# 31 short warming matmuls in place of 15 long ones ahead of a graph-attention kernel

## The chip, the cores and the metric

The kernel runs on one core of a Trainium2 chip. The metric is the device time of one execution in microseconds (us). A TensorE "record" below is one instruction of TensorE as the profile lists it: a weight load (LDWEIGHTS, shown under PEld) or a matmul (MATMUL, shown under PE). A matmul of the program on 32-bit floats comes out as two weight loads and two matmuls, so as four records.

## The reference

The input `x` is 128 graphs of 128 nodes with 768 features, `adj` a 128x128 weighted adjacency per graph. Everything is float32.

```python
h = jnp.maximum(_layernorm(x, axis=-1), 0.0)
x = x + _L0_gnn_ref(h, adj, L0_gnn_Wq, L0_gnn_bq, L0_gnn_Wk, L0_gnn_bk, L0_gnn_Wv, L0_gnn_bv, L0_gnn_beta)
...
q = _split_heads(input_graph @ Wq + bq)
k = _split_heads(input_graph @ Wk + bk)
v = _split_heads(input_graph @ Wv + bv)
scores = jnp.einsum('bhqd,bhkd->bhqk', q, k) / jnp.sqrt(jnp.asarray(HD, input_graph.dtype))
adj_e = adj[:, None, :, :]
scores = scores + beta * adj_e
scores = jnp.where(adj_e > 0, scores, jnp.asarray(-9000000000000000.0, scores.dtype))
probs = jax.nn.softmax(scores, axis=-1)
out = jnp.einsum('bhqk,bhkd->bhqd', probs, v)
```

There are 12 heads of 64 features (`HD`), and `_split_heads` gives each head its own axis.

## The kernel before, in words

The 128 graphs are worked in 32 groups of four (`G` = 0 to 31). For each group there are three "slices" of projections: `qk0` (queries and keys of heads 0 to 5), `v`, and `qk1` (the other queries and keys). In group 0 the projections are plain matrix products (`plain_slice`, line 1048, its first row `first_row`, line 1265). From group 1 on a slice is made of 15 block products (`PRODUCTS`) and each of these of seven inner products (`product`, line 681), every one issued as two matmuls that write the upper and the lower 64 partitions. The right-hand sides of these products were added up once at the start (`prepare`), are kept in DRAM, and are streamed back in a ring of six buffers (`load_T`, the tiles `T_qk` and `T_v`); ten of them stay resident. VectorE, ScalarE and GpSimd add the products up (line 704 and following), decode them, and do masks, exponentials and divisions. The scores (line 776) and the weighting of the values (line 855) of one group are woven between the products of the next.

The order of the work is written out: a table of due times (`TABLE`, with `FIRST`, `SECOND`, `LAST` for the ends) is counted in products, 45 to a group, and every group from the second on issues the same list of instructions on each engine. So TensorE's program is one long list without loops, in which the same stretch comes again once per group.

The change lies at the very start. `direct` first issues the loads of the first two graphs and the weights, and GpSimd writes a 128x128 identity into `ident`. Then `fill(WARM)` puts matmuls of the identity with itself into one PSUM bank, whose result nobody reads: they keep TensorE busy until the first normalised row is there. `rows_1` takes the statistics of a graph on VectorE (line 1089 and following) and `rows_2` scales its row (line 1107), transposes it on TensorE (line 1112), puts one or two more matmuls of `fill` behind each transpose (`FILL`), and takes the result away on ScalarE (line 1118). After that come the products of the first row (line 1265).

Of the kernel before, what the change touches and what calls it, by code (L numbers as in the profile page):

```python
# [18 lines left out]
P = 128  # L19
# [12 lines left out]
@with_exitstack  # L32
def kernel(
    ctx: ExitStack,
    tc: tile.TileContext,
    x: bass.AP,
    adj: bass.AP,
    wq: bass.AP,
    bq: bass.AP,
    wk: bass.AP,  # L40
    bk: bass.AP,
    wv: bass.AP,
    bv: bass.AP,
    beta: bass.AP,
    out: bass.AP,
):

    nc = tc.nc
    keep = ctx.enter_context(tc.tile_pool(name="keep", bufs=1))
    bad = keep.tile([1, 1], I32, name="bad")
    args = (x, adj, wq, bq, wk, bk, wv, bv, beta, out)
    direct(tc, *args, bad)
    again = nc.values_load(bad[0:1, 0:1])
    with tc.If(again > 0):
        general(tc, *args)  # L60
# [43 lines left out]


SC_AT = 1
WARM = 15
FILL = (1, 1, 2)


# [116 lines left out]
def direct(ctx, tc, x, adj, wq, bq, wk, bk, wv, bv, beta, out, bad):  # L227
# [10 lines left out]
    nc = tc.nc  # L238
    B, N, D = x.shape
    HD = D // HEADS  # L240
# [30 lines left out]
    def flat(lo, hi):  # L271
        return sbig[:, lo:hi]
# [32 lines left out]
    ident = flat(spot, spot + P)  # L305
# [772 lines left out]
    def rows_1(g, h):  # L1078

        t = xg[0, g].rearrange("p b f -> p (b f)")
        if not h:
            first["st", g] = stat.tile([P, 2, nc.vector.BN_STATS_DIM], F32, tag="strow_0", name=f"strow0_{g}", bufs=2)
        s = first["st", g]
        with ExitStack() as behind:
            if g:
                behind.enter_context(tc.issue_after(first[("ve", "dve")[h]].ins))
            nc.vector.bn_stats(s[:, h, :], t[:, h * VH:(h + 1) * VH])
        if not h:  # L1090
            return None
        mv = stat.tile([P, nc.vector.BN_AGGR_DIM], F32, tag="mvrow_0", name=f"mvrow0_{g}", bufs=2)
        nc.vector.bn_aggr(mv, s)
        ve = stat.tile([P, 1], F32, tag="verow_0", name=f"verow0_{g}", bufs=2)
        first["ve"] = nc.vector.tensor_scalar(ve, mv[:, 1:2], EPS, None, op0=ALU.add)
        r = stat.tile([P, 1], F32, tag="rsrow", name=f"rsrow_{g}", bufs=2)
        nc.gpsimd.tensor_tensor(r, ve, nhalf, ALU.pow)
        return mv, r

    def rows_2(g, mv, r, ks=range(3)):  # L1100

        v = xg[0, g].rearrange("p b (c j) -> p c b j", c=NC)
        for k in ks:
            if not k:
                first["rows", g] = work.tile([P, 3, 2, P], F32, tag="e", name=f"rows_{g}", bufs=EB)
            n = first["rows", g][:, k]
            first["dve"] = nc.vector.tensor_scalar(n.rearrange("p c (b j) -> p c b j", b=NB), v[:, 2 * k:2 * k + 2], mv[:, 0:1], r, op0=ALU.subtract,
                                                   op1=ALU.mult)
            bank = take()
            p = bank[:, 0, 0:H2].rearrange("p (c i) -> p c i", c=2)  # L1110
            for c in range(2):
                nc.tensor.transpose(p[:, c, :], n[:, c, :], ident)
            if not g:
                fill(FILL[k])
            if not g:
                home_A(0, f"A0{k}")
            t = A[0, f"A0{k}"][:, :, g * N:(g + 1) * N]
            first["relu"] = nc.scalar.activation(t, p, AF.Relu)
            give(bank)


    warm = take()

    def fill(count):
        for _ in range(count):
            nc.tensor.matmul(warm[:, 0, 0:P], ident, ident, start=True, stop=True)

    fill(WARM)
    got = [rows_1(0, h) for h in range(2)]
    rows_1(1, 0)  # L1130
    rows_2(0, *got[1])
# [369 lines left out]
```

## Time and profile before

| What | Value |
|---|---|
| time, median of 3 runs | 2667.34 us (2666.55 to 2667.99) |
| span of the profiled execution, first to last instruction | 2664.1 us |
| what the median has beyond that span | 3.2 us |
| TensorE busy | 2644.1 us, 99% of the span, 52041 matmuls and as many weight loads |
| VectorE, ScalarE, GpSimd busy | 81%, 66%, 79% |
| mean rate of the DMA engines | 277 GB/s |
| mean granted TensorE clock | 0.998 |

The profile gives one execution; it has no time of its own beside the span, so the 3.2 us are what lies before the first and after the last instruction, as far as that execution and the median are alike. Matmuls are pipelined, and the end of one is modelled: a matmul that is listed with 273 ns is followed by the next one long before. The step from start to start is what counts. "Idle before" is the time in which the engine had nothing in hand, with what ended it; "issue" stands where no semaphore explains it.

### The profile page before, as it was taken

What the parts mean: (1) busy time and instruction counts of PE and PEld (TensorE: products, weight loads), DVE (VectorE), ACT (ScalarE), POOL (GpSimd) and SP (SyncE); (2) the same over time, 40 slices, a digit from 0 to 9 for tenths busy, and PEclk for the clock granted to TensorE, in tenths of its full rate; (3) what the DMA queues carried; (4) which work ended last, traced back from release to release, by engine and by line L of the source; (5) the groups of instructions that cost most, each with busy time, mean ns of one, the idle gap of its engine ahead of it and who ended that gap; (6) DMA issues with size and microseconds to landing.
All of it is one profiled execution on the core that took longest, in us unless ns stands there. A gap on an engine that the chain in (4) does not pass through costs nothing.

```text
span 2664.1 us, 121442 instructions
## 1 busy us (share of the span) xinstructions
PE 2644.1 (99%) x52041; PEld 2564.2 (96%) x52041; DVE 2165.8 (81%) x2702; ACT 1755.1 (66%) x4608; POOL 2097.8 (79%) x3043
## 2 busy tenths in 40 slices
PE   9999999999999999999999999999999999999998
PEld 8799999999999999999999999999999999999997
DVE  7878887878888788887788887888877888778876
ACT  2567766677666677666777666776667776667654
POOL 5877778877779777788777797777887777887774
PEclk9999999999999999999999999999999999999999
DMA  8899999998989999999999899999899898999885
GB/s 254 276 281 279 282 284 278 283 292 267 293 281 279 287 277 284 281 281 280 289 269 288 281 281 282 288 275 285 279 278 292 268 291 279 276 286 282 256 253 165
DMA packets 531572, 736.65 MB, mean 277 GB/s; under 512 B 106444, under 2 KB 371160, under 8 KB 531032
## 3 DMA queue, kind: packets, MB, share of 16 engines
q1 hardware_dynamic: 530384, 728.06, 88.5%
q8 instruction: 411, 6.73, 1.0%
q14 instruction: 129, 1.06, 0.1%
q10 hardware_dynamic: 648, 0.79, 0.1%
HBM read 662.22 MB, written 66.51 MB: 274 GB/s over the span
## 4 chain that ended last, share of the span: by engine, by line
PE 94%; DVE 1%; DMA 0%; issue 0%; ACT 0%; SPq 0%; DVEq 0%; ACTq 0%
PE pair L681 80%; PE pair L776 7%; PE pair L855 6%; PE pair L1048 1%; DVE home L704 0%; DMA x<-in_x_dram 0%; DMA T_qk<-kept_qk 0%; PE pair L926 0%; DVE e L789 0%; DVE prep_qk L403 0%; ACT e L836 0%; DVE res_qk L403 0%; PE pair L947 0%; DVE e L931 0%; ACT e L933 0%
## 5 line engine op out<-in xcount | busy, mean ns | idle before, releaser
L704 DVE TENSOR_TENSOR home<-home,pair 128x896 f32<-128x896 f32 x836 | 880.0, 1077 | 220.5 <-PE pair L681 179.8
L681 PE MATMUL pair<-sbig,T_qk 128*64 128x128 f32 x13020 | 827.6, 274 | 2.3 <-DVE home L704 1.2
L681 PEld LDWEIGHTS pair<-sbig,T_qk 128*64 128x64 f32 x13020 | 702.5, 137 | 19.9 <-issue 12.1
L739 POOL TENSOR_TENSOR home<-home 128x256 f32<-128x256 f32 x308 | 266.1, 864 | 320.0 <-DVE home L704 319.7
L681 PE MATMUL pair<-T_v,sbig 128*64 128x128 f32 x7812 | 457.8, 273 | 1.6 <-ACT home L716 0.6
L681 PE MATMUL pair<-A,T_qk 128*64 128x128 f32 x6944 | 445.6, 273 | 0.9 <-issue 0.9
L681 PEld LDWEIGHTS pair<-T_v,sbig 128*64 128x64 f32 x7812 | 430.7, 137 | 8.4 <-ACT e L836 4.8
L855 PE MATMUL pair<-v,e 128*64 128x65 f32 x6048 | 403.5, 221 | 0.0
L836 ACT ACTIVATE e<-e,sm 128x64 f32<-128x64 f32 x1512 | 381.7, 341 | 7.4 <-DVE sm L824 6.1
L681 PEld LDWEIGHTS pair<-A,T_qk 128*64 128x64 f32 x6944 | 384.6, 137 | 1.5 <-issue 1.5
L855 PEld LDWEIGHTS pair<-v,e 128*64 128x64 f32 x6048 | 362.2, 137 | 3.2
L724 ACT ACTIVATE home<-pair 128x640 f32<-128x640 f32 x340 | 240.6, 708 | 188.5 <-PE pair L681 187.2
L681 PE MATMUL pair<-sbig,res_qk 128*64 128x128 f32 x4340 | 312.3, 273 | 0.4
L742 POOL TENSOR_TENSOR home<-home 128x256 f32<-128x256 f32 x308 | 269.7, 876 | 24.1
L885 ACT ACTIVATE sm<-pair,tiny 128x8 f32<-128x8 f32 x189 | 50.8, 269 | 329.5 <-PE pair L855 329.5
L789 DVE SCALAR_TENSOR_TENSOR e<-pair,biasT 128x1024 f32<-128x1024 f32 x189 | 229.4, 1214 | 34.1 <-PE pair L776 33.0
L740 POOL TENSOR_TENSOR home<-home 128x256 f32<-128x256 f32 x308 | 228.2, 741 | 24.1
L681 PEld LDWEIGHTS pair<-sbig,res_qk 128*64 128x64 f32 x4340 | 238.0, 137 | 1.4 <-DVE home L704 1.3
L560 ACT ACTIVATE x<-x,block 128x192 f32<-128x192 f32 x480 | 222.6, 540 | 0.0
L726 ACT ACTIVATE home<-pair,bqk 128x128 f32<-128x128 f32 x680 | 214.3, 377 | 0.0
L798 ACT ACTIVATE e<-e 128x1024 f32<-128x1024 f32 x189 | 196.1, 1055 | 21.8 <-DVE e L789 14.0
L741 POOL TENSOR_TENSOR home<-home 128x128 f32<-128x128 f32 x308 | 175.6, 570 | 24.2
(208 smaller groups left out, 4401.6 us busy)
## 6 DMA issues: line engine op xcount, KB each, us to landing
T_qk<-kept_qk SPq DMA_DIRECT2D x713, 448.0 KB
T_v<-kept_v SPq DMA_DIRECT2D x372, 448.0 KB
xo<-in_x_dram SPq DMA_DIRECT2D x190, 256.0 KB
out_dram<-xo SPq DMA_DIRECT2D x189, 256.0 KB
x<-in_x_dram SPq DMA_DIRECT2D x248, 192.0 KB
sbig<-in_x_dram SPq DMA_DIRECT2D x116, 384.0 KB
kept_qk<-prep_qk SPq DMA_DIRECT2D x23, 448.0 KB
adj<-in_adj_dram SPq DMA_DIRECT2D x128, 64.0 KB
```

Source lines behind the costliest of these rows:

```text
L560: nc.scalar.activation(t, t, AF.Relu, bias=shift[G, n], scale=rstd[G, n])
L681: nc.tensor.matmul(p[q:q + HD, at, :], lhs[:, q:q + HD], rhs, start=(first and at % 4 == 0), stop=True, skip_group_check=True)
L704: nc.vector.tensor_tensor(t, t, p[:, 0:7], op)
L724: nc.scalar.activation(t[:, 0:5], p[:, 0:5], AF.Copy, scale=float(sign))
L726: nc.scalar.activation(t[:, at], p[:, at], AF.Identity, bias=bqk[:, of, oc:oc + 1], scale=float(sign))
L739: e.tensor_tensor(t[:, 1:4:2], t[:, 1:4:2], twice(5), ALU.add)
L740: e.tensor_tensor(t[:, 2:5:2], t[:, 2:5:2], twice(1), ALU.add)
L742: e.tensor_tensor(t[:, 0:7:6], t[:, 0:7:6], twice(2), ALU.add)
L789: nc.vector.scalar_tensor_tensor(e[:, :, at], ps[:, :, at], SCORE_CAP * ISCALE, bias[:, :, at], op0=ALU.min, op1=ALU.add)
L798: nc.scalar.activation(e, e, AF.Exp, scale=1.0 / ISCALE)
L836: nc.scalar.activation(o[:, r, b, 0:HD], pa[:, r, b, 0:HD], AF.Copy, scale=t[:, 1, r, b:b + 1])
L855: nc.tensor.matmul(pa[q:q + HD, 2 * g + i, :], k[:, q:q + HD], vt[G, "v", r, h // 4][:, 4 * g + h % 4, :], start=True, stop=True, skip_gro ...
```

## The change

`WARM` goes from 15 to 31, `fill` gets a width, and the first call uses 64 columns (`HD`) where it had 128 (`P`). The weights of each of these matmuls are still the whole 128x128 identity. The calls `fill(FILL[k])` in `rows_2` keep 128 columns. In records: 31 times 4 are 124, in place of 60, so that everything that TensorE runs later stands 64 records further along in its program.

```diff
-WARM = 15
+WARM = 31
 FILL = (1, 1, 2)
...
-    def fill(count):
+    def fill(count, width=P):
         for _ in range(count):
-            nc.tensor.matmul(warm[:, 0, 0:P], ident, ident, start=True, stop=True)
-
-    fill(WARM)
+            nc.tensor.matmul(warm[:, 0, 0:width], ident, ident[:, 0:width], start=True, stop=True)
+
+    fill(WARM, HD)
     got = [rows_1(0, h) for h in range(2)]
```

## The prediction, as it was put on record

> **What bounds the kernel now.** I read the page first: the engine table, the clock row, the DMA queues, and the chain that ended last.
>
> ```profile
> span 2664.1 us, 121442 instructions
> PE 2644.1 (99%) x52041; PEld 2564.2 (96%) x52041; DVE 2165.8 (81%) x2702; ACT 1755.1 (66%) x4608; POOL 2097.8 (79%) x3043
> ...
> PEclk9999999999999999999999999999999999999999
> ...
> q8 instruction: 411, 6.73, 1.0%
> ...
> PE 94%; DVE 1%; DMA 0%; issue 0%; ACT 0%; SPq 0%; DVEq 0%; ACTq 0%
> ```
>
> TensorE (PE) sets the time: 99% busy, 94% of the chain, at full clock. So the change can act in two ways only: through when TensorE gets through its first microseconds, and through anything that hangs on where an instruction stands in TensorE's list. The row of q8 speaks for the second. This queue moved 411 packets of 6.73 MB / 411 = 16.4 KB, of kind "instruction", and TensorE ran 104082 matmuls and weight loads: 253 for each packet, 256 once its semaphore instructions are counted. I take q8 for TensorE's own program, fetched in blocks of 256 records.
>
> Then the long view of the chain, in order of time. The same stretch of 284 matmuls opens every group; six of these rows:
>
> ```profile
> 171.94 15.65 PE pair L681 x284
> ...
> 1063.68 15.65 PE pair L681 x284
> 1145.49 15.65 PE pair L681 x284
> ...
> 1552.26 15.65 PE pair L681 x284
> ...
> 2120.69 15.65 PE pair L681 x284
> ...
> 2527.99 15.65 PE pair L681 x284
> ```
>
> The first eleven groups take (1063.68 - 171.94) / 11 = 81.07 us each, the last eighteen (2527.99 - 1063.68) / 18 = 81.35 us, though every group issues the same list. The later ones lose 0.28 x 18 = 5.1 us. The timeline of weight loads shows where most of it goes: breaks put down to "issue", with no semaphore behind them. Breaks of 0.17 us that come back in every group are left aside; of the others none lies before 1134 us in a full group.
>
> ```profile
> 1134.82 0.13 PEld L776 LDWEIGHTS pair<-home 64*64 64x64 f32 x1 [0.49 <-issue]
> ...
> 1199.04 0.63 PEld L681 LDWEIGHTS pair<-A,T_qk 128*64 128x64 f32 x12 [0.54 <-issue]
> ...
> 1298.21 0.79 PEld L681 LDWEIGHTS pair<-T_v,sbig 128*64 128x64 f32 x14 [0.25 <-issue]
> ...
> 1443.49 0.79 PEld L681 LDWEIGHTS pair<-A,T_qk 128*64 128x64 f32 x14 [0.48 <-issue]
> ...
> 1606.36 0.74 PEld L681 LDWEIGHTS pair<-A,T_qk 128*64 128x64 f32 x13 [0.43 <-issue]
> ...
> 1949.48 0.52 PEld L681 LDWEIGHTS pair<-T_v,sbig 128*64 128x64 f32 x9 [0.28 <-issue]
> ...
> 2193.71 0.41 PEld L681 LDWEIGHTS pair<-T_v,sbig 128*64 128x64 f32 x7 [0.49 <-issue]
> ...
> 2356.34 0.35 PEld L681 LDWEIGHTS pair<-T_v,sbig 128*64 128x64 f32 x6 [0.18 <-issue]
> ...
> 2438.52 0.42 PEld L681 LDWEIGHTS pair<-T_v,sbig 128*64 128x64 f32 x8 [0.39 <-issue]
> ```
>
> They sum to 3.53 us. What lies between two of them, counted by stretches (start and end, sum, then busy time and count of PE and PEld, VectorE, ScalarE, GpSimd, clock, DMA share, GB/s), and the semaphore instructions on TensorE's main line:
>
> ```profile
> 1134.84:1199.02 64.18, 63.80 (x1265) 62.30 (x1265) 52.69 (x61) 42.92 (x107) 52.94 (x77) 1.00 0.91 278
> 1199.06:1298.20 99.14, 99.14 (x2027) 96.96 (x2028) 80.18 (x99) 68.38 (x187) 78.21 (x113) 1.00 0.92 282
> 1443.52:1606.34 162.82, 162.54 (x3293) 159.21 (x3293) 133.22 (x159) 111.48 (x294) 131.28 (x189) 1.00 0.92 281
> ...
> L681 PEldq EVENT_SEMAPHORE  x990: 51/51/1724, 120.0 to 2645.6; - x198
> ```
>
> There are 990 semaphore instructions in 2526 us, so about 0.4 per us. That makes 2530 + 25, 4055 + 39 and 6586 + 64 records: 2555, 4094 and 6650, against 10, 16 and 26 times 256 (2560, 4096, 6656). The breaks stand at one place modulo 256: they are boundaries of blocks, at which the next block was not yet there. One packet of q8 lies in the 1.2 us from 1132.3 us, just ahead of the break at 1134.82:
>
> ```profile
> q8 instruction: 1, 0.02, 5.0%
> ```
>
> **The change part by part.** First the 32 more matmul records and 32 more weight loads of the fill. The rows, from the timeline of the first 21 us, the source view of the fill, and the chain:
>
> ```profile
> 1.49 5.80 PE L1126 MATMUL pair<-sbig 128*128 128x128 f32 x30 [1.49 <-POOL sbig masks.py:199]
> 7.62 0.20 PEld L1112 LDWEIGHTS pair<-sbig,rows 128*128 128x128 f32 x2 [0.52 <-DVE rows L1107]
> 7.62 0.44 PE L1112 MATMUL pair<-sbig,rows 128*128 128x128 f32 x2 [0.33 <-DVE rows L1107]
> 9.22 1.06 PE L1265 MATMUL pair<-A,sbig 128*128 128x128 f32 x8
> 20.45 0.29 PE L475 MATMUL pair<-st,sbig 128*64 128x16 f32 x4 [1.04 <-DVE st L464]
> ...
> L1126 PE MATMUL pair<-sbig x38: 274/421/582, 1.5 to 9.1; 128*128 128x128 f32 x38
> ...
> 107.81 0.23 PE pair L855 x8
> ```
>
> Once warm, eight matmuls of 128 columns start within 1.06 - 0.275 us, 0.112 us apart (0.275 being the shortest of one, 274 ns). The fill's 30 take 5.80 us, 0.19 us each, since most run at half speed (median 421 ns against 274). Half the columns should take half the step, if the weight load (128 columns as before) fits into it. By itself such a load takes about 0.06 us: the two of line 1112 span 0.20 us, of which the second is some 0.14. That is just the warm half step of 0.056 us, and the rows of 65 columns run at 0.23 / 8 = 0.029 us each, two at a time, 0.058 us a step. So 62 half steps are 31 of the old steps: one more than 30, by 0.11 us if warm. The fill would end near 7.4 in place of 7.29 us. TensorE then stands idle until 7.62 us, when VectorE's scaled row comes (0.33 us), and this covers it: cost 0. If the cover were gone, the first transpose would be late, and behind it lines 1118 and 1265. Upper end: weight load and matmul one after the other, as long as a whole old step. Then 62 steps take 2 x 5.80 us or rather less, as the clock opens after the same 4.5 us: 21 slow ones in 4.4 us, 41 at 0.112 us in 4.6 us, an end at 10.5 us, 2.9 us late. The wait at 20.45 us for line 464, which goes by VectorE and a load, takes 1.04 of that, the one of 0.33 us is already in it: at most +1.9 us. A gain here is excluded: nothing waits for the end of the fill but a row that comes later.
>
> Second, the 64 records. They move every block boundary 64 records up the schedule. A group is 81.05 us or about 13 blocks, so a record is 81.05 / 13 / 256 = 0.0244 us on average, and the boundary comes 1.56 us earlier in the work. Where do the breaks stand within a group? 1199.04 - 1145.49 = 53.55 us in one, 1606.36 - 1552.26 = 54.10 us five groups later: 0.11 us of drift a group. At the other place 1134.82 - 1063.68 = 71.14 and 2193.71 - 2120.69 = 73.02 us, thirteen groups on: 0.14 us a group. At some 0.12 us a group, 1.56 us are 13 groups. So group G will have its boundaries where group G - 13 has them now. The two bad places are entered in the twelfth and thirteenth of the 29 groups; they will be entered 13 groups later. Of the nine breaks, the four up to 1443.49 us (0.49 + 0.54 + 0.25 + 0.48 = 1.76 us) come back, at the end of the run; the five from 1606.36 on (1.77 us) fall off it. Bounds of this term: -1.8 by the rows; if all the 5.1 us are such breaks, half of it, -2.6.
>
> The price is that the first 13 groups put their boundaries where none has been. Each group has 13 of them, so 169 fetches are at unvisited places, against 29 x 13 = 377 that cost 3.53 us: at that mean 1.6 us. To do better than the mean I look at what a bad place is: few microseconds for the 256 records of a block, while the DMA engines are full. Five blocks of a group without breaks, two bad ones first, then the three shortest or fullest of those newly visited:
>
> ```profile
> 300.88:306.28 5.40, 5.40 (x128) 5.22 (x128) 4.91 (x6) 5.08 (x10) 1.70 (x3) 1.00 1.00 341
> 318.15:323.61 5.46, 5.46 (x133) 5.12 (x128) 2.17 (x5) 3.71 (x12) 4.99 (x9) 1.00 0.98 324
> 303.79:309.44 5.65, 5.65 (x134) 5.65 (x132) 5.10 (x8) 5.29 (x15) 3.39 (x4) 1.00 1.01 372
> 322.19:327.85 5.66, 5.66 (x134) 5.49 (x128) 3.69 (x5) 5.48 (x15) 5.19 (x9) 1.00 0.94 300
> 292.28:297.71 5.43, 5.43 (x130) 5.09 (x128) 5.43 (x6) 5.37 (x16) 5.12 (x6) 1.00 0.92 276
> ```
>
> Bad are 5.40 and 5.46 us at a DMA share of 1.00 and 0.98. Only the third is as full (1.01), and it leaves 0.2 us more, which takes away about half of a break of 0.2 to 0.5 us; the fourth and fifth are less full. I take +1.0 us: one place, some 0.15 us in half of 13 groups. Lower end 0; upper end a new place that breaks in all 13 groups by 0.5 us, +6.5.
>
> Sum: 0 - 1.8 + 1.0 = -0.8 us. On the span that is 2663.3; the median lies 3.2 us above the span of the profiled execution, which the change doesn't touch: **2666.5 us**, 0.03% less. What a measurement of this kernel can tell from no change is about 0.2%, 5.3 us.
>
> [...]
>
> **The rivals.** (a) All breaks go and no new ones come: -3.5 by the rows, -5.1 by the groups' lengths, 2662.2 to 2663.8 us. For it: eleven groups run without any. Against: blocks as short as the bad ones lie among the new places. (b) The other side: the block that ends 56 us into a group (303.79 to 309.44) is late in all of the first 13 groups, at 0.3 to 0.5 us: +3.9 to +6.5, less 1.8: 2669.4 to 2672.0, and over 2672.7 only if the block at 322.19 joins it. It decides as soon as the fetch takes 0.2 us longer there than at the bad places. For it: the fullest DMA share of all; against: the longer block. (c) The fill gets longer, because the weight load doesn't fit into the half step, or the clock opens later for short matmuls: up to +1.9 - 0.8: 2668.4 us. Against: the rows with 65 columns. (d) Blocks are always there in time, the breaks hang on something else in the later part of the run, and the shift moves nothing: 2667.3 us. Against: the counts. [...]
>
> **How the numbers follow.** Forecast (net -2.5 to +1.5): 0.68. (a) 0.14, (b) 0.10, (c) 0.04, (d) 0.04. Range: down to 2662.5 for (a), up to 2671.0 for most of (b). Faster by over 0.2% is below 2662.0, just past the far end of (a), with the scatter of the median (0.7 us to either side) some of it: 0.06. Slower is above 2672.7, the part of (b) with both blocks: 0.06. The rest, 0.88, is no change.
>
> **What would show it.** Fill: 62 matmuls at line 1126 that end by 7.6 us, line 1112 still starting at 7.62 with a wait for VectorE. Fetch: breaks by "issue" at the two old places (53.6 and 71.1 us into a group) only from the 25th of the 29 groups on, at most four or five; few or small ones near 56 us in the first 13 groups; all a multiple of 256 records apart. Groups at 81.05 us where there is no break. It is wrong if breaks stay at the same groups as now, if a new place breaks in nearly every group, or if the median leaves the range.

## The result, and the profile after

The changed kernel takes 2673.36 us (median of 13 runs, 2670.75 to 2675.08), the kernel before 2667.74 us beside it (13 runs, 2666.49 to 2669.09): a ratio of 1.0019, 95% interval 1.0011 to 1.0027, so 5.6 us slower. The forecast of 2666.5 us was wrong in its sign, and its range of 2662.5 to 2671.0 us doesn't hold the time. The two profiled executions differ by 2670.6 - 2664.1 = 6.5 us in their spans, and this is what has to be found. It is 0.9 us more than the medians show: in every run with a span on record the time is 1.7 to 1.9 us above it, so the execution of before that was profiled took about 2665.9 us, 1.8 less than the median here, and the changed one, with 2672.43 us, 0.9 less than its own. (Of the 3.2 us that were taken for time outside the span, only some 1.8 are that.)

First the page of the changed kernel: span, engines, the instruction queue and the chain that ended last.

```profile
span 2670.6 us, 121506 instructions
PE 2650.7 (99%) x52073; PEld 2572.3 (96%) x52073; DVE 2164.7 (81%) x2702; ACT 1755.1 (66%) x4608; POOL 2097.8 (79%) x3043
...
q8 instruction: 412, 6.75, 1.0%
...
PE pair L681 80%; PE pair L776 7%; PE pair L855 6%; PE pair L1126 1%; PE pair L1265 0%; POOL prep_qk L386 0%; POOL prep_qk L385 0%; DVE home L704 0%; DMA sbig<-in_L_gnn_Wk_dram 0%; DMA kept_qk<-prep_qk 0%; DVE prep_qk L403 0%; POOL A L590 0%; POOL prep_v L385 0%; POOL prep_v L386 0%; POOL rstd L496 0%
```

TensorE still sets the time, and its busy time has grown by the whole difference, 2650.7 - 2644.1 = 6.6 us, with 32 matmuls more. VectorE, ScalarE and GpSimd work as long as before. The chain of before could be followed back only to 93.8 us, so the first part of this one can't be compared with it. In order of time it begins with line 1126, the fill, which holds 1%. It goes on through the first row on TensorE until 31 us and through the preparation on VectorE and GpSimd (the lines 403, 385 and 386), and is back on TensorE at 134 us; so what is late at the start is handed on through the preparation.

Now the timeline of TensorE's matmuls in the first 29 us. Columns: start, length, engine, line, operation, tile, number of matmuls in a row, and in brackets the idle time ahead of it.

```profile
1.49 13.49 PE L1126 MATMUL pair<-sbig 128*128 128x64 f32 x62 [1.49 <-POOL sbig masks.py:199]
14.77 0.64 PE L1112 MATMUL pair<-sbig,rows 128*128 128x128 f32 x2
...
17.76 1.76 PE L1265 MATMUL pair<-A,sbig 128*128 128x128 f32 x8
19.35 0.38 PE L1112 MATMUL pair<-sbig,rows 128*128 128x128 f32 x2
...
20.68 1.06 PE L1265 MATMUL pair<-A,sbig 128*128 128x128 f32 x8
...
28.38 0.29 PE L475 MATMUL pair<-st,sbig 128*64 128x16 f32 x4
```

The fill takes 13.49 us for 62 matmuls of half the columns, where it took 5.80 us for 30 whole ones. The last one has 0.42 us (421 ns, below), so the step is (13.49 - 0.42) / 61 = 0.214 us; it is 0.213 to 0.214 us from the second step to the last. The first transpose (line 1112) starts at 14.77 us instead of 7.62, 7.15 us late, with no wait ahead of it: the row from VectorE has long been there, and the transpose waits for the fill. The row behind it runs slowly too: line 1265 takes 1.76 us for eight matmuls at 17.76 us and 1.06 us at 20.68 us, as it did at once before. The trace's first record of full speed for TensorE's clock stands at 19.22 us, in place of 6.11 us in the kernel before; the matmuls show the same change of speed between the rows of 17.76 and 19.35 us. (The granted clock of a stretch is listed as 1.00 also ahead of the first record, so here the steps have to be read, not that column.) So the fill is long and it doesn't warm. By line 475 the delay is 28.38 - 20.45 = 7.93 us; it was 21.57 - 12.54 = 9.03 us at the last transpose of the first row, and line 475's wait for VectorE, 1.04 us, has gone into it.

The source view of line 1126, by length of one instruction in ns (shortest, median, longest), first of the kernel before, then of the changed one; and line 1112 before:

```profile
L1126 PEld LDWEIGHTS pair<-sbig x38: 190/333/333, 1.5 to 9.0; 128*128 128x128 f32 x38
...
L1112 PEld LDWEIGHTS pair<-sbig,rows x12: 138/142/143, 7.6 to 12.5; 128*128 128x128 f32 x12
```

```profile
L1126 PEld LDWEIGHTS pair<-sbig x70: 286/333/337, 1.5 to 17.3; 128*128 128x128 f32 x70
L1126 PE MATMUL pair<-sbig x70: 421/421/473, 1.5 to 17.5; 128*128 128x64 f32 x62, 128*128 128x128 f32 x8
```

Matmuls of 64 columns are as long as those of 128, 421 ns in the median, and the weight load is as long as ever, 333 ns at the low speed. At line 1126 it is listed with 190 ns at full speed and 333 ns at the low one, but at line 1112, at full speed, with 138 to 143 ns, the load from which the prediction took its price.

Last, the later part. The stretch of 284 matmuls that opens a group, in the chain in order of time, and the breaks at block boundaries from the timeline of the weight loads:

```profile
179.75 15.65 PE pair L681 x284
...
342.28 15.65 PE pair L681 x284
...
1073.14 15.65 PE pair L681 x284
...
2370.13 15.65 PE pair L681 x284
2453.27 15.65 PE pair L681 x284
2535.06 15.65 PE pair L681 x284
```

```profile
236.14 0.13 PEld L681 LDWEIGHTS pair<-sbig,res_qk 128*64 128x64 f32 x1 [0.30 <-issue]
...
399.21 0.13 PEld L855 LDWEIGHTS pair<-v,e 128*64 128x64 f32 x1 [0.59 <-issue]
...
2425.39 1.17 PEld L681 LDWEIGHTS pair<-A,T_qk 128*64 128x64 f32 x21 [1.71 <-issue]
...
2507.39 1.07 PEld L681 LDWEIGHTS pair<-A,T_qk 128*64 128x64 f32 x20 [0.75 <-issue]
```

The changed kernel is 179.75 - 171.94 = 7.81 us behind at the first of these places, 1073.14 - 1063.68 = 9.46 us at the twelfth and 2535.06 - 2527.99 = 7.07 us at the thirtieth. So the first eleven groups lost 1.65 us, the later eighteen won 2.39 us back, and between the first place and the thirtieth the changed kernel won 0.74 us. New breaks stand 236.14 - 179.75 = 56.4 and 399.21 - 342.28 = 56.9 us into a group, early in the run; the old places, 2425.39 - 2370.13 = 55.3 and 2507.39 - 2453.27 = 54.1 us in, are reached in the 28th and 29th. What the change costs is made in the first 20 us of the run.

That these breaks are late fetches can be read from the packets. The largest ends at 2425.39 us. One packet of q8 lies in the stretch from 2423.0 to 2424.1 us, and none from there to the end of the break:

```profile
q8 instruction: 1, 0.02, 5.2%
```

By the packets' times in the trace it landed at 2423.98 us, 1.41 us before TensorE went on. The four breaks of 0.3 us and more here, and eight of the nine that the prediction lists for the kernel before (all but the one of 0.18 us), end 1.3 to 1.7 us after their block's packet has landed; at the boundaries without a break TensorE enters the block 3.4 to 3.5 us after that in the median.

### The profile page after: what moved, and what is told of

The parts are those of the page before. It is cut to its first block, busy times and chain, and to the rows that moved or that the text cites. A ratio compares the mean times of both kernels' runs of the same rounds, so it can differ in the third digit from the quotient of the medians.

```text
span 2670.6 us, 121506 instructions
## 1 busy us (share of the span) xinstructions
PE 2650.7 (99%) x52073; PEld 2572.3 (96%) x52073; DVE 2164.7 (81%) x2702; ACT 1755.1 (66%) x4608; POOL 2097.8 (79%) x3043
## 3 DMA queue, kind: packets, MB, share of 16 engines
q14 instruction: 129, 1.06, 0.1%
## 4 chain that ended last, share of the span: by engine, by line
PE 95%; POOL 2%; DVE 2%; DMA 1%; issue 1%; ACT 0%; SPq 0%; DVEq 0%; POOLq 0%; ACTq 0%
PE pair L681 80%; PE pair L776 7%; PE pair L855 6%; PE pair L1126 1%; PE pair L1265 0%; POOL prep_qk L386 0%; POOL prep_qk L385 0%; DVE home L704 0%; DMA sbig<-in_L_gnn_Wk_dram 0%; DMA kept_qk<-prep_qk 0%; DVE prep_qk L403 0%; POOL A L590 0%; POOL prep_v L385 0%; POOL prep_v L386 0%; POOL rstd L496 0%
## 5 line engine op out<-in xcount | busy, mean ns | idle before, releaser
L681 PEld LDWEIGHTS pair<-sbig,T_qk 128*64 128x64 f32 x13020 | 703.0, 137 | 19.7 <-issue 12.1
```

The source lines that it names most:

```text
L681: nc.tensor.matmul(p[q:q + HD, at, :], lhs[:, q:q + HD], rhs, start=(first and at % 4 == 0), stop=True, skip_group_check=True)
```

## The experiments

Theory A: the weight load of 128 columns sets the step of a matmul with fewer columns, 0.213 us at the low speed, and an array that streams half of the time doesn't open the clock; the shift of 64 records does next to nothing. Rival B: the start is small, and the shift costs the time. Rival E: load and matmul go in turns, so that the step is their sum. F and G stand for two views of the breaks: F, a place in a group decides whether the fetch of a block is late; G, it is chance.

**The shift alone.** The fill of before; in group 0, in the wait ahead of line 475, 16 matmuls of one column whose result nobody reads, 64 records.

```diff
+        for _ in range(16 if G == 0 else 0):
+            nc.tensor.matmul(bank[0:1, 1, 0:1], ident[:, 0:1], ident[:, 0:1], start=True, stop=True)
```

> The fill is the old one (15 of 128 columns); 16 matmuls of one column with one column of weights, 64 records, stand later, where TensorE waits 1.04 us at line 475 about 20 us into the run. So every block boundary of all full groups lies as in the changed kernel. Theory A (the loss of 5.6 us is made in the fill, the shift alone is worth -0.7 us, the 7.81 to 7.07 us by which the changed kernel is behind at 172 us and at 2528 us): 2667.0 us, within 2666 to 2668; breaks where the changed kernel has them, in the first 9 groups about 56 us into the group and two large ones in the last two. Theory B (the loss is made by the shifted block boundaries): 2673 us.

Measured: 2664.89 us against 2665.98, ratio 0.9998 (0.9988 to 1.0008). The chain of this kernel at the same three places (line 681 stands at 683 here):

```profile
172.20 15.65 PE pair L683 x284
...
1066.13 15.65 PE pair L683 x284
...
2528.06 15.65 PE pair L683 x284
```

The first eleven groups take 893.93 us, 2.2 more than before, the later eighteen 1461.93 us, 2.4 less: the same exchange as in the changed kernel, and nothing is left of it at the end. B falls; what costs is the fill. The expected breaks came at the expected places (56.4 and 56.9 us into two of the first groups, 54.0 and 72.3 us into two late ones), but also 74.8 to 76.1 us into three of the first eleven groups, 0.32 to 0.62 us each, where the changed kernel has none.

**What sets the step.** Three fills of 31 with the same shift of 64 records: 128 columns, 32 columns, and 64 columns with weights of only 64 columns.

```diff
-WARM = 15
+WARM = 31
```

> 31 matmuls of the old 128 columns, 124 records: the same shift as in the changed kernel, a longer fill, but a dense one. Theory A: the clock opens near 6.1 us as before, 21 steps of 0.213 and 41 of 0.112 us end at 10.6 us, first transpose 3.0 us late, 1.1 us given back at 20.45 us: +1.9 us at 172 us, the shift -0.7 us: 2668.9 us, less than the changed kernel although twice the columns are streamed. Theory D (the number of matmuls or records ahead of the row counts, whatever their width): as the changed kernel, 2673 us.

```diff
-    fill(WARM, HD)
+    fill(WARM, 32)
```

> As the changed kernel, but 32 columns in each of the 31 matmuls. Theory A (the load of 128 columns of weights alone sets the step at half clock): step 0.213 us again, the fill ends at 14.7 us as with 64 columns, and the clock opens some 4.5 us after the first dense matmuls, near 19 us: about 2672 us. Theory E (load and matmul take turns: 0.107 us for the load, 0.053 us for 32 columns): step 0.160 us, the fill ends at 11.4 us.

```diff
-            nc.tensor.matmul(warm[:, 0, 0:width], ident, ident[:, 0:width], start=True, stop=True)
+            nc.tensor.matmul(warm[0:width, 0, 0:width], ident[:, 0:width], ident[:, 0:width], start=True, stop=True)
```

> 31 matmuls of 64 columns as in the changed kernel, but each with 64 columns of weights instead of 128. Theory A (the load of 128 columns of weights sets the step of 0.213 us, and a matmul of half that length leaves the array half idle): load and matmul are both halved, the step is 0.107 us and dense, the clock opens near 6 us, the fill ends near 7.3 us: no loss in the first 172 us, the shift -0.7 us: 2667.0 us. Theory E (a weight load and a short matmul take turns, whatever their length): step 0.107 us for the matmul and 0.05 to 0.107 us for the load in turn, 0.16 to 0.21 us, the fill ends at 11 to 14 us and the clock opens late: 2670 to 2673 us.

Measured, as the fill stands in the timeline and in the source view, for 128 columns, for 32, and for the half weights:

```profile
1.49 8.52 PE L1126 MATMUL pair<-sbig 128*128 128x128 f32 x62 [1.49 <-POOL sbig masks.py:199]
9.85 0.38 PE L1112 MATMUL pair<-sbig,rows 128*128 128x128 f32 x2
```

```profile
1.49 13.44 PE L1126 MATMUL pair<-sbig 128*128 128x32 f32 x62 [1.49 <-POOL sbig masks.py:199]
14.74 0.67 PE L1112 MATMUL pair<-sbig,rows 128*128 128x128 f32 x2
```

```profile
1.50 6.34 PE L1126 MATMUL pair<-sbig 128*64 128x64 f32 x62 [1.50 <-POOL sbig masks.py:199]
7.77 0.44 PE L1112 MATMUL pair<-sbig,rows 128*128 128x128 f32 x2
...
L1126 PEld LDWEIGHTS pair<-sbig x70: 138/227/232, 1.5 to 9.2; 128*64 128x64 f32 x62, 128*128 128x128 f32 x8
```

A quarter of the columns takes as long as half of them, 13.44 against 13.49 us, so it is the load alone that sets the step, and E falls: with load and matmul in turns the 32 columns would have been shorter. With whole streams the same 62 loads end after 8.52 us, five us sooner than the "short" ones, because the clock opens (at 4.33 us by its record, sooner than the 6.1 us expected) and the step falls from 0.213 to 0.111 us. With half the weights the step is 0.107 and then 0.058 us, and the fill ends at 7.84 us: only here do half the columns take half the step. The times: 2666.54 us for the whole columns (ratio 1.0001, 0.9991 to 1.001), 2664.22 us for the half weights (0.9994, 0.9984 to 1.0003), 2674.23 us for the 32 columns (one run). So what the change cost is gone once the weights are halved with the columns, and neither the kernel with whole columns nor the one with half weights can be told from the kernel before.

**What opens the clock.** The count of before with 64 columns, and 31 of 96 columns:

```diff
-    fill(WARM)
+    fill(WARM, HD)
```

> 15 matmuls of 64 columns, 60 records as before the change, no shift. Theory A (a matmul of 64 columns behind a whole weight load takes the same 0.213 us as one of 128, and such a fill does not open the clock, which opens some 4.5 us after the first dense matmuls): 30 steps end near 7.9 us, 0.3 us late; the clock stays at half until about 12.4 us; first transposes and products lose about 1.9 us more, the wait at 20.45 us takes 1.1 back: +1.1 us, 2668.8 us. Theory C (only the length of the fill counts, not the clock): +0.3 us that the wait takes back, 2667.7 us. If a step were really half as long, the fill would end at 4.7 us and the clock would be the question alone.

```diff
-    fill(WARM, HD)
+    fill(WARM, 96)
```

> 96 columns in each of the 31 matmuls. Theory A: step 0.213 us at half clock, with the array streaming for 0.160 of it. Theory E: 0.267 us. On the clock: if it opens by how much of the time the array streams, and three quarters are enough, it opens near 6 us and the kernel is where 31 of 128 columns was (fill until 9.7 us, 1.1 us behind at 172 us); if three quarters are not enough, it opens near 19 us as with 64 columns (7.8 us behind).

The timelines, of 15 with 64 columns and of 31 with 96:

```profile
1.49 6.67 PE L1126 MATMUL pair<-sbig 128*128 128x64 f32 x30 [1.49 <-POOL sbig masks.py:199]
7.95 0.63 PE L1112 MATMUL pair<-sbig,rows 128*128 128x128 f32 x2
```

```profile
1.49 9.67 PE L1126 MATMUL pair<-sbig 128*128 128x96 f32 x62 [1.49 <-POOL sbig masks.py:199]
10.99 0.38 PE L1112 MATMUL pair<-sbig,rows 128*128 128x128 f32 x2
```

At the low speed both have the step of 0.213 us, which is also the step of whole columns, so by an estimate from these equal steps the array streams 64 / 128 = 50% and 96 / 128 = 75% of the time. At 75% the clock opens at 6.77 us; at 50% it hasn't opened when the fill ends, the first transposes take 0.63 us as in the changed kernel, and it opens at 11.86 us, 3.9 us after whole streams have begun. In the changed kernel that was 19.22 - 14.77 = 4.45 us. The short fill alone would not show that half streams fail to open the clock, since whole streams took up to 6.2 us to do it (last section); the 13 us of the changed kernel and of the 32 columns do. The two kernels also part the two factors. 15 half streams cost little: 2667.3 us, ratio 1.0005 (0.9995 to 1.0014), 0.75 us behind at the place of 171.9 us. 31 at 75% cost 2.20 us there (2670.24 us, one run). Only many loads, all of them at the low speed, cost 7.8.

Does a half-streamed array also close a clock that is open? And what is the warming worth at all? Two more, each one run:

```diff
     fill(WARM)
+    fill(31, HD)
```

> The 15 matmuls of 128 columns first, as before, and then the 31 of 64 columns. If a half-streamed array only fails to open the clock but doesn't close it, the second part goes at 62 steps of 0.111 us: an end at 7.3 + 6.9 = 14.2 us, the first transpose at 14.3, the row behind it at full speed (line 1265 at 15.9), and the place of 171.9 us at about 177.5 (14.3 - 7.6, less the 1.0 of line 475's wait). If the half-streamed array closes the clock again, steps of 0.213 us come back within the second part, its end is up to 20.5 us, and the place is at 178 to 185. If instead the slow steps of the changed kernel had nothing to do with the clock, the steps are 0.213 us from the first of the second part on: an end at 20.5 us.

```diff
-WARM = 15
+WARM = 0
```

> No warming matmuls at all. By the theory the first row then runs at half speed, as in the changed kernel, but starts at 7.6 us: line 1112 takes 0.6 instead of 0.44 us, line 1265 1.76 instead of 1.06, in all 1.9 us later at 12 us (9.0 - 7.15 of the changed kernel), of which the wait at line 475 gives back about 1.0: the place of 171.9 us at 172.8, and the whole 1 us (plus what the 60 records in the other direction do to the fetch, up to 1 either way) above the kernel before. So the changed kernel, with the place at 179.7, would be 7 us worse than no warming at all. If the late start of the clock did not matter, the place is at 171.9.

The timelines, with both fills (line 1265 stands at 1266) and with none:

```profile
1.49 12.31 PE L1126 MATMUL pair<-sbig 128*128 128x128 f32 x92 [1.49 <-POOL sbig masks.py:199]
...
15.20 1.06 PE L1266 MATMUL pair<-A,sbig 128*128 128x128 f32 x8
```

```profile
7.35 1.12 PE L1112 MATMUL pair<-sbig,rows 128*128 128x128 f32 x4 [5.06 <-DVE rows L1107]
...
9.97 1.56 PE L1265 MATMUL pair<-A,sbig 128*128 128x128 f32 x8
```

Once open, the clock stays open through the half streams: 92 matmuls with 92 loads end sooner than the 62 of the changed kernel (13.80 against 14.98 us), and the row behind them runs at full speed. But for one step of 0.058 us, where the two parts meet, the short ones step 0.110 to 0.113 us there: at full speed, too, a load of 128 columns sets the step. So the changed kernel's steps of 0.213 us are that load with the clock closed. This kernel stands 4.96 us behind at the place of 171.9 us, which was forecast as 5.6; its program is shifted by 124 records against the kernel before, and with that its first eleven groups lose 5.5 us, of which the later eighteen win 3.2 back (see below). It takes 2672.67 us.

Without any fill the place is 0.82 us behind (0.9 was expected), and the kernel takes 2667.9 us in the one run. The warming of before earns at most that 0.8 us; that of the changed kernel loses 7.8 against it.

**What the fetch does, with the boundaries held.** A group has 3323 records, five short of 13 blocks of 256 (the trace of before has 104082 matmuls and loads and 1114 semaphore instructions of TensorE for 411 packets of q8, 256 to a packet); a matmul of one column in each group makes 3327, so that the boundaries stay at nearly one place. Its result is overwritten. The second kernel has 49 matmuls of one column more at 20 us, so that the boundaries are held at a bad place.

```diff
+        if sl == "qk0" and G > 1 and n == order_of(G, sl)[0]:
+            nc.tensor.matmul(p[0:1, 0, 0:1], b[:, 0, 0:1], b[:, 0, 0:1], start=True, stop=True, skip_group_check=True)
```

> The kernel before with one more matmul of one column (4 records, about 0.06 us) at the start of each of the 30 groups from the third on. A group then has 3327 records in place of 3323, against 13 blocks of 256 = 3328, so that the boundaries of the blocks hardly move from group to group and stay where the first groups have them, which ran without breaks. Theory F (the breaks are late blocks of TensorE's program, decided by where in a group the boundaries lie): no breaks at boundaries, the 4 us of them gone, 1.8 us paid for the matmuls: -2 to -3 us, 0.999 of the kernel before. Theory G (the breaks come with the later part of the run, whatever the place): they stay, +1.8 us.

> The kernel with the extra matmul per group, and 49 matmuls of one column (196 records, 2.5 us, of which the wait at 20 us hides 1.0) once, about 20 us into the run. The boundaries stay all through the run where the kernel before has them in its 13th to 18th full group, with the breaks. Theory F: breaks at 53 and 71 us into most groups, 0.3 us a group on the mean, +9 us against the kernel with the extra matmuls alone, +6 to +8 us against the kernel before: 1.002 to 1.003. Theory G: +1.5 us against the kernel with the extra matmuls alone, and breaks in later groups only.

All breaks of the first kernel (those of 0.17 us left aside), then three of the second, from the timelines of the weight loads:

```profile
717.93 0.68 PEld L683 LDWEIGHTS pair<-A,T_qk 128*64 128x64 f32 x12 [0.18 <-issue]
...
1225.07 0.52 PEld L683 LDWEIGHTS pair<-res_v,A 128*64 128x64 f32 x9 [0.22 <-issue]
...
1451.15 0.74 PEld L683 LDWEIGHTS pair<-A,T_qk 128*64 128x64 f32 x13 [0.48 <-issue]
```

```profile
390.33 1.28 PEld L685 LDWEIGHTS pair<-A,T_qk 128*64 128x64 f32 x23 [0.47 <-issue]
...
1390.30 1.83 PEld L685 LDWEIGHTS pair<-T_v,sbig 128*64 128x64 f32 x33 [1.46 <-issue]
...
1700.23 0.90 PEld L685 LDWEIGHTS pair<-A,T_qk 128*64 128x64 f32 x16 [0.88 <-issue]
```

Held at a clean place there are 3 breaks with 0.88 us in all, held at a bad one 17 with 9.1 us, over the whole run. By chance the two would have had alike: G falls, and F holds as to the place. In the second, 15 of the 17 breaks are longer than 0.2 us, and they too end 1.3 to 1.6 us after their packet has landed. In which group a bad place breaks, and for how long, is not set by the place: the kernel with 15 of 64 columns has the boundaries of the kernel before, but three breaks at boundaries before 1000 us (0.22, 0.15 and 0.12 us), where that one has none, and one of 1.79 us. The second takes 2682.64 us (ratio 1.0058, 1.0045 to 1.0072), 12.8 more than the first, and 14.7 more than the kernel before where 6 to 8 were expected. Of the 12.1 us between the two profiled executions, 2.1 lie before the first full group: the 98 steps of 0.025 us of the 49 matmuls and a clock that fell for a while behind them (last section), less what the wait took. 9.6 lie in the groups, of which 8.2 are the breaks. The first, at 2669.84 us (1.0008, 0.9999 to 1.0017), gains nothing over the kernel before in spite of them, since the added matmul costs 0.26 us in each group where 0.06 had been expected: a group without a break takes 81.31 instead of 81.05 us. This expectation was missed.

If that price came from the head of the product, where the matmul stands ahead of the first operand, it should fall inside the product:

```diff
+            if sl == "qk0" and G > 1 and at == 4 and n == order_of(G, sl)[0]:
+                nc.tensor.matmul(p[0:1, at, 0:1], lhs[:, 0:1], rhs[:, 0:1], start=True, stop=True, skip_group_check=True)
```

> The one-column matmul that holds the block boundaries at one place of a group, as in the steady runs, but in the middle of the first product of a group instead of ahead of it, with the operands that the array works on there; nothing is left out. If its 0.26 us a group came from standing at the head of a product, ahead of the first of its operands, it costs here only its two steps of 0.025 us and at most two loads of 0.03 us, 0.05 to 0.11 us a group, 1.5 to 3.3 us in the run, and since the breaks at boundaries fall from 4.2 to about 0.9 us the kernel takes 2664.5 to 2666.5 where the kernel before takes 2667.7: ratio 0.9988 to 0.9996. If the 0.26 us come from the change of tile shape itself, it takes about 2670, ratio 1.0008, and the place doesn't matter.

It doesn't: 2669.89 us, ratio 1.0012 (1.0003 to 1.0021), though only one break of 0.19 us is left in the run. The source view of the added matmul:

```profile
L681 PEld LDWEIGHTS pair<-sbig,T_qk x60: 78/81/83, 207.8 to 2566.9; 128*1 128x1 f32 x60
L681 PE MATMUL pair<-sbig,T_qk x60: 162/163/165, 207.8 to 2566.9; 128*1 128x1 f32 x60
its engine sat idle before it (us, times) until:
  issue: 5.1, 30
```

Each is preceded by 5.1 / 30 = 0.17 us of idle time put down to "issue", at either place. The same 0.17 us stand where the shape of the weights changes between lines 776 and 681, in the changed kernel too:

```profile
227.64 0.43 PEld L776 LDWEIGHTS pair<-home 64*64 64x64 f32 x16 [0.17 <-issue]
...
228.67 1.73 PEld L681 LDWEIGHTS pair<-sbig,T_qk 128*64 128x64 f32 x32 [0.17 <-issue]
```

So the price is most likely the change of shape; that was seen at two places, not tried with a pad of the neighbours' shape. A version that is faster beyond doubt than both kernels was not found: held at a clean place the breaks fall from 3.5 to under 1 us, but the pads cost 30 x 0.26 = 7.8, and the two kernels with them are 1.9 and 3.0 us slower than the kernel before.

## Why the prediction was wrong, point by point

**What bounds the kernel: right.** The 6.5 us came through TensorE's first microseconds, one of the two ways named, and the chain now begins with line 1126.

**The fill: the step that failed.** "Half the columns should take half the step, if the weight load (128 columns as before) fits into it. By itself such a load takes about 0.06 us." It doesn't fit. The 0.06 us were read from line 1112, whose instructions are transposes: one record each in place of two, with loads of 138 to 143 ns, while the load of line 1126 itself stands in the trace of before with 190 ns at full speed. The other evidence, the rows of 65 columns (line 855), have weights of 64 columns, as line 681 has, and these loads take 137 ns in the mean. Two lines of the page of before, with the mean behind the busy time:

```profile
L681 PEld LDWEIGHTS pair<-sbig,T_qk 128*64 128x64 f32 x13020 | 702.5, 137 | 19.9 <-issue 12.1
...
L855 PEld LDWEIGHTS pair<-v,e 128*64 128x64 f32 x6048 | 362.2, 137 | 3.2
```

So a step of 0.058 us showed that a load of 64 columns fits into it, and nothing on one of 128. By this comparison, with rows of before alone, a load of line 1126 was 0.053 us longer than one of 64 columns, and the runs give the steps: 0.058 us for 64 columns and 0.111 us for 128 with the clock open, 0.107 and 0.213 us with it closed. With the load of 128 columns kept and the clock closed, the step was 0.213 us for streams of 128, 96, 64 and 32 columns alike, so halving the stream halved nothing.

**The bound of that step: wrong as well.** The prediction did price a load and a matmul of a whole old step, but "as the clock opens after the same 4.5 us", and came to 10.5 us for the end and +1.9 us. With the clock open from 6.8 us, 62 loads of 128 columns do end near there (31 of 96 columns, one run: first transpose at 10.99 us, 2.20 us behind at 171.9 us). But the half-streamed array never opened it. So 62 x 0.213 = 13.2 us, the first transpose 7.15 us late, another 1.9 us lost in the row behind it at low speed (9.03 us at its last transpose), 1.1 us got back at line 475: 7.9 us there, 7.8 at 171.9 us. About 2.2 us of this are the longer fill with a clock that opens on the way, as with 96 columns (1.1 us with 128, whose clock opened sooner), the other 5.6 the closed clock. In the changed kernel TensorE's rows show no idle time from 1.49 to 14.77 us, and the clock didn't open in these 13.28 us, so being busy in the profile's sense was not enough here.

**The cover: right, and far too small.** The wait of 0.33 us would have hidden the expected 0.1 us. It nearly does so for the half weights: their fill's last matmul starts at 7.62 us and ends, as modelled, at 7.84, the transpose starts at 7.77 us, 0.15 us late, and at the place of 171.9 us that kernel is not behind (171.91 us).

**The 64 records: the mechanism right, the number luck.** Forecast -0.8 us, measured -0.74 between the places of 171.9 and 2528 us. But six kernels on record have this shift, and the same difference against the kernel before is -0.19 us with the shift alone, +0.36 with 128 columns, -2.79 with the half weights, -0.11 with 32 columns, +1.48 with 96, one execution each; the kernel with 15 of 64 columns, without any shift, has +0.86. So a term of this size doesn't stand out from one execution to the next. What all six do alike is to lose in the first eleven groups (0.73 to 3.18 us) and to win in the later eighteen (0.55 to 3.52 us), as was forecast. The new place was forecast 56 us into a group with +1.0 us; the breaks of the first nine groups stand at 56.4 to 56.9 us and sum to 0.98 us (0.30, 0.59 and one of 0.09). The other five kernels break there too, and all five also 74.6 to 76.4 us into a group, behind the block that ends at 327.85 us, which the sum left out. The old places come back late in the run, though in two groups rather than four, with larger breaks: 1.71 + 0.75 us against 1.76 forecast. The groups' lengths, +1.65 and -2.39 us, move more than the breaks by themselves, which sum to 3.45 us here and about 3.5 before; what the other part is was not traced.

**The rivals.** (c) was the case: the weight load doesn't fit and the clock opens later, both named in one sentence; but its price was bounded at +1.9 us instead of +7.8, and its chance set to 0.04. (a) falls: five breaks stay. (b) falls for this shift, as the new place broke in three of the groups, but it is no fancy: by 124 records instead of 64 the first eleven groups lost 5.5 us with a break in each, 73 to 75 us in for ten of them. (d) falls by the kernels with held boundaries and by the packets. Most blocks came in time in these kernels, but not all: 3 breaks with 0.9 us and 17 with 9.1 us, with the boundaries held at two places.

**The range.** It was spent on the fetch, up and down, and its upper end had no part of the fill. The 0.3 us of cover next to a step of unknown size, 62 times over, was the place for it: every 0.02 us of error in that step is 1.2 us.

## What to carry to other kernels

In these runs the step of the fill's matmuls and of line 1265's was the larger of their stream and their weight load (with the clock open 0.111 us for 64 columns behind a load of 128, 0.216 us for 256 columns behind the same load), so before narrowing a stream, find the row of the load of that same operation and width, not of a neighbour that merely looks like it. Here the matmuls meant to warm the clock opened it where they kept the array streaming, with whole columns (after 2.8 to 6.2 us) or with weights cut along with them (the step went from 0.107 to 0.058 us within the fill); at half the stream they ran 13 us without opening it, and warmed nothing; at three quarters it opened after 5.3 us (one run). And where a change moves the length of an engine's program, measure the shift by itself with instructions in an idle stretch; here that took the larger suspect away in one run.

## What the runs showed of the hardware that was not expected

- The clock opened between 2.8 us (31 of 128 columns, 1.49 to 4.33) and 6.2 us (the shift alone, 1.50 to 7.71) after whole streams began, one execution each. These two have the same fill for its first 30 matmuls, so with the same start the opening varied by 3.4 us.
- It closed in the middle of work. In the kernel held at a bad place, 49 matmuls of one column took TensorE from 19.2 to 21.6 us; the clock's record then shows half speed from 23.2 to 26.6 us, while TensorE was busy without a break, on matmuls of 256 columns but for four of 16 (6.00 of the 6.00 us from 22 us on). That the short matmuls closed it is not shown: it is one execution, and 16 of them at the same place (the shift alone) were followed by no such record. The stretch of 22 to 28 us has a granted clock of 0.72 (start and end, sum, busy time and count of the five engines, clock, DMA share, GB/s):

```profile
22.00:28.00 6.00, 6.00 (x23) 4.59 (x24) 1.72 (x8) 0.67 (x2) 2.45 (x4) 0.72 1.05 214
```

- Half streams held open a clock that they did not open in 13 us by themselves: 62 of them ran 6.9 us at full speed behind 15 whole ones (one run).
- A matmul of one column cost a step of 0.025 us among its like, but 0.26 us alone between matmuls of another shape.
- A block of TensorE's program came so late that TensorE stood idle for up to 1.8 us (15 of 64 columns), against 0.54 us at most in the trace of before:

```profile
1545.07 1.07 PEld L681 LDWEIGHTS pair<-T_v,sbig 128*64 128x64 f32 x20 [1.79 <-issue]
```
